# Adding the experts' results for every other sequence on GpSimd in place of TensorE and VectorE, in the last stage of a Mamba and mixture-of-experts block

## The chip, the cores and the metric

The kernel runs on one core of one Trainium2 chip. The metric is the device time of one execution in microseconds (us), as the median over several runs. A profile is one further execution, recorded by the hardware profiler; its span runs from the first to the last instruction of the program, and its times are counted from the span's start. The core has five engines with a queue of instructions each: TensorE (PE; the loads of its weights appear as PEld), VectorE (DVE), ScalarE (ACT), GpSimd (POOL) and SyncE (SP). SP, ACT and POOL also issue DMAs.

## The reference

The input x has 8 sequences of 512 tokens with 128 channels. The block has two halves: an attention-like part of four Mamba-2 layers, and a feed-forward part with a shared expert and eight routed experts of which each token takes two. Each half is modulated by vectors made from a condition c.

```python
h = _layernorm(x, axis=-1) * (1 + ca) + sa
x = x + ga * _L0_attn_ref(h, ...)              # four Mamba-2 layers
h = _layernorm(x, axis=-1) * (1 + cb) + sb
x = x + gb * _L0_ffn_ref(h, ...)               # experts

# in _L0_ffn_ref
shared = jnp.maximum(normed @ sw1 + sb1, 0.0) @ sw2 + sb2
scores, idx = jax.lax.top_k(probs, TOPK)       # two experts of eight for each token
w = scores / (jnp.sum(scores, axis=-1, keepdims=True) + 1e-06)
...
routed = jnp.einsum('teo,te->to', eo, comb)    # the two experts' results, weighted and added
return shared + routed.reshape(b, s, -1)
```

All values are float32.

## The kernel before, in words

All sequences stay in SBUF as tiles xs[b] of 128 partitions by 4 x 128 values. The Mamba layers come first and take most of the time, with the routing of the first sequences beside the last layer. Each routed token is written as a row to a list of its expert in DRAM (`xg`), once for each of its two experts. Then come 39 tiles of 256 rows each: `fetch` loads the expert's weights and the rows, `turn` transposes them, `hidden` makes the hidden layer, and `combine` makes the expert's result, adds its bias (L1218), multiplies each row by its weight (L1220) and scatters it to a DRAM table `yg` with indirect DMAs of GpSimd (L487). In `yg` the first result of token t stands in row t, its second in row T + t, where T is the number of all tokens. Beside these tiles, `fold` adds the shared expert's part to xs[b] and loads the gate gb of sequence b to `gbs[b]`, 128 values that are the same on every partition.

The last stage begins when the last scatter has landed. For each of the 8 sequences b it loads y1[b] (the first results) by a DMA of SP and y2[b] (the second results) by a DMA of ACT, both 128 x 512 values, 256 KB (L1269). The loads of all sequences are issued ahead of the additions. Two sequences share one tile of the pool `xbp`. After that a second loop goes over the sequences:

- TensorE adds: a matmul of the identity matrix with y1[b], and one with y2[b] on top of it, in one bank of PSUM, `sum2` (L1275, L1276). The pool of banks has three.
- VectorE multiplies the sum in PSUM by gb, broadcast over the four tokens of a partition, and writes the product over y1[b] (L1278).
- VectorE adds the product to xs[b] (L1281).
- SP stores xs[b] to the output (L1282), 256 KB.

The order of instructions on PE, DVE, ACT and SP is the order of the program text, as it stands in this part of the kernel (`tc.manual_schedule` names all engines but Pool). On GpSimd the order is set by the scheduler of the tile framework. Waits between engines come from the framework: an instruction waits for the semaphores of what made its inputs, and each engine runs its own instructions in order. SP therefore issues the stores in the order of the sequences, and a store that waits holds the later ones.

Of the kernel before, what the change touches and what calls it, by code (L numbers as in the profile page):

```python
# [15 lines left out]
P = 128  # L16
# [8 lines left out]
def adaln_mamba_moe(  # L25
# [27 lines left out]
    nc = tc.nc  # L53
    B, L, DM = x.shape
# [4 lines left out]
    NC = L // Q  # L59
# [39 lines left out]
    ident = const.tile([P, P], F32, name="ident")  # L99
# [39 lines left out]
    def step(gen):  # L139

        return gen is not None and next(gen, gen) is not gen
# [71 lines left out]
    hTs, hp, xp, xs = {}, {}, {}, {}  # L213
# [271 lines left out]
    def scatter(to, of, ix, group):  # L485

        i = nc.gpsimd.indirect_dma_start(  # L487
            out=to, out_offset=bass.IndirectOffsetOnAxis(ap=ix, axis=0), in_=of, in_offset=None
        )
        tc.declare_no_dep(i.ins, group=group, reason="the rows that they write are distinct")  # L490
        tc.add_to_no_dep_group(group, i.ins)
# [12 lines left out]
    def pbank(name):  # L504
        return psP.tile([P, 512], F32, tag="p", name=name)
# [61 lines left out]
    def serve():  # L567
        nonlocal serving
        if not step(serving):
            serving = None  # L570

    with ExitStack() as actx:
# [422 lines left out]
        for t in range(-NC * LEAD - EARLY, NI + 4):  # L995
            p = t + NC * LEAD
# [101 lines left out]
    gbs = {}  # L1098
    fgb = ctx.enter_context(tc.tile_pool(name="fgb", bufs=B))

    def fold(b):

        gbs[b] = fgb.tile([P, DM], F32, tag="gb", name=f"gb{b}")
        nc.sync.dma_start(gbs[b], mods[b, 3].partition_broadcast(P))
        yield
        nc.vector.tensor_add(accs[b], accs[b], b2.unsqueeze(1).to_broadcast([P, NC, DM]))
        yield
        nc.vector.tensor_mul(accs[b], accs[b], gbs[b].unsqueeze(1).to_broadcast([P, NC, DM]))
        yield
        nc.vector.tensor_add(xs[b], xs[b], accs[b])  # L1110
# [53 lines left out]
    def fetch(j):  # L1164
        to = tab["to"]
        e = nc.sync.value_load(to[:1, 0, j : j + 1], min_val=0, max_val=E - 1)
        r = nc.sync.value_load(to[:1, 1, j : j + 1], min_val=0, max_val=E * ER)
        w1x[j] = fw3.tile([P, FH], F32, tag="w1", name=f"w1_{j}")
        nc.sync.dma_start(w1x[j], ew1[bass.ds(e, 1)].rearrange("o d h -> d (o h)"))
        w2x[j] = fw3.tile([P, FK, DM], F32, tag="w2", name=f"w2_{j}")  # L1170
        nc.sync.dma_start(w2x[j], ew2[bass.ds(e, 1)].rearrange("o (k p) d -> p (o k) d", p=P))

        b2x[j] = fw3.tile([P, DM], F32, tag="b2", name=f"b2_{j}")
        nc.sync.dma_start(b2x[j], eb2[bass.ds(e, 1)].rearrange("o d -> (o d)").partition_broadcast(P))

        def rest():
            rows_in[j] = fw3.tile([P, 2, RW], F32, tag="rows", name=f"rows{j}")
            nc.sync.dma_start(rows_in[j], xg[bass.ds(r, TT), :].rearrange("(p s) w -> p s w", s=2))

        return rest  # L1180

    def turn(j):
        pt = psT.tile([P, 2, P], F32, tag="t", name=f"pt{j}")
        for s in range(2):
            nc.tensor.transpose(pt[:, s, :], rows_in[j][:, s, :DM], ident)  # L1185
        xts[j] = fh.tile([P, TT], F32, tag="xt", name=f"xt{j}")
        nc.scalar.activation(xts[j], pt.rearrange("p s t -> p (s t)"), AF.Copy, scale=nw)

    def hidden(j):
        hds[j] = hd = fh.tile([P, FK, TT], F32, tag="hd", name=f"hd{j}")  # L1190
        xt, w1 = xts.pop(j), w1x.pop(j)
        for half in range(2):
            ph = pbank(f"ph{j}_{half}").rearrange("p (k t) -> p k t", t=TT)
            ks = range(half * FK // 2, (half + 1) * FK // 2)
            for i, k in enumerate(ks):
                nc.tensor.matmul(ph[:, i, :], w1[:, k * P : (k + 1) * P], xt, start=True, stop=True)  # L1196
            for i, k in enumerate(ks):
                bias = tab["b1"][:, j, k : k + 1]
                if half:
                    nc.vector.tensor_scalar(hd[:, k, :], ph[:, i, :], bias, 0.0, ALU.add, ALU.max)  # L1200
                else:
                    nc.scalar.activation(hd[:, k, :], ph[:, i, :], AF.Relu, bias=bias)  # L1202

    def combine(j):
        hd, w2, rows = hds.pop(j), w2x.pop(j), rows_in.pop(j)
        pe = banks[-1](f"pe{j}")[:, : 2 * DM].rearrange("p (s d) -> p s d", s=2)
        for s in range(2):
            for k in range(FK):
                nc.tensor.matmul(  # L1209
                    pe[:, s, :], hd[:, k, s * P : (s + 1) * P], w2[:, k, :], start=(k == 0), stop=(k == FK - 1)  # L1210
                )
        ix = fh.tile([P, 2], mybir.dt.uint32, tag="ix", name=f"ix_{j}")

        own = fh.tile([P, 2], F32, tag="own", name=f"own{j}")
        nc.vector.tensor_scalar(own, rows[:, :, DM + 1], float(2 * T), float(j * TT), ALU.is_ge, ALU.mult)
        nc.vector.tensor_add(ix, own, rows[:, :, DM + 1])
        y = fh.tile([P, 2, DM], F32, tag="y", name=f"y{j}")
        nc.vector.tensor_add(y, pe, b2x.pop(j).unsqueeze(1).to_broadcast([P, 2, DM]))  # L1218
        for s in range(2):
            nc.vector.tensor_scalar_mul(y[:, s, :], y[:, s, :], rows[:, s, DM : DM + 1])  # L1220
        for s in range(2):
            scatter(yg, y[:, s, :], ix[:, s : s + 1], "results")

    with tc.manual_schedule(engines={*tc.nc.engines} - {mybir.EngineType.Pool}):
        tail = list(gens.values())
        fetched = []
        table = None
        while tail or serving or scatters or table or not tab:
            for g in list(tail):
                if not step(g):  # L1230
                    tail.remove(g)
            while scatters:
                scatter(*scatters.pop(0)[1:])
            serve()
            for g in list(tail):
                if not step(g):
                    tail.remove(g)
            serve()
            if len(taken) == len(sets) + 1 and not tab:
                table = tables()  # L1240
            if not step(table):
                table = None
            if not fetched and "to" in tab:
                fetched = [fetch(j) for j in range(3)]
            serve()
        for rest in fetched:
            rest()
        turn(0)
        turn(1)
        hidden(0)  # L1250
        folding = [fold(b) for b in range(B)]
        for j in range(NT):
            if j + 3 < NT:
                fetch(j + 3)()
            if j + 1 < NT:
                hidden(j + 1)
            if j + 2 < NT:
                turn(j + 2)
            combine(j)
            if folding and not step(folding[0]):  # L1260
                del folding[0]

        y1, y2 = {}, {}
        for b in range(B):
            both = xbp.tile([P, NX, L], F32, tag="xbc", name=f"y{b}") if b % 2 == 0 else both
            for c, (eng, y) in enumerate(((nc.sync, y1), (nc.scalar, y2))):
                y[b] = both[:, 2 * (b % 2) + c, :]
                r = c * T + b * L
                eng.dma_start(  # L1269
                    y[b].rearrange("p (s d) -> p s d", d=DM),  # L1270
                    yg[r : r + L, :].rearrange("(p s) d -> p s d", s=NC),
                )
        for b in range(B):
            sum2 = pbank(f"sum{b}")
            nc.tensor.matmul(sum2, ident, y1[b], start=True, stop=False)  # L1275
            nc.tensor.matmul(sum2, ident, y2[b], start=False, stop=True)  # L1276
            y = y1[b].rearrange("p (s d) -> p s d", d=DM)
            nc.vector.tensor_mul(  # L1278
                y, sum2.rearrange("p (s d) -> p s d", d=DM), gbs[b].unsqueeze(1).to_broadcast([P, NC, DM])
            )  # L1280
            nc.vector.tensor_add(xs[b], xs[b], y)  # L1281
            nc.sync.dma_start(out[b].rearrange("(s p) d -> p s d", p=P), xs[b])  # L1282


# [49 lines left out]
```

## Time and profile before

| | |
|---|---|
| median of 3 runs | 1150.44 us (1149.92 to 1153.31) |
| the profiled execution | 1151.86 us |
| its span | 1150.2 us (1150.15 unrounded) |
| granted TensorE clock, mean | 0.93 |
| busy: PE, DVE, ACT, POOL | 967.3, 859.0, 761.5, 856.3 us |
| last scatter issued / first y load issued | 1122.60 / 1124.85 |
| first sum begins / last x ready | 1129.57 / 1146.76 |
| loads of y, stores of x in the last stage | 16 and 8, of 256 KB each |

A profile's busy time is that of the whole span; what the change touches is the last 25 us, so it is read in windows, in the chain of waits (which is followed backwards from the last instruction to whatever released each one) and in the timeline of single instructions. The groups of instructions give counts and mean durations, and a group's line names the engine, the operation, output<-inputs and their shapes.

### The profile page before, as it was taken

The page shows a single profiled execution, that of the slowest core. Times are in us where ns is not written, and L with a number is a line of the kernel's source. Part 1 is how long each engine was busy: PE and PEld are TensorE (multiplying, and loading weights), DVE is VectorE, ACT ScalarE, POOL GpSimd, SP SyncE. Part 2 cuts the span into 40 slices and gives each one's busy share as a digit, 9 for nine tenths or more (in the row PEclk, how much of TensorE's full clock was granted, in tenths as well). Part 3 has the DMA queues.
Part 4 walks back from the last instruction along what each step waited for, and adds up shares of the span by engine and source line. Part 5 has one row for each costly group of instructions (what it writes and reads, how often), then busy time and mean ns, then how long its engine had stood idle before and what let it go on. Part 6 is the DMA issues. An engine that isn't in the chain of part 4 may idle for free. (4 is left out here: it accounts for less than half of the span.)

```text
span 1150.2 us, 21566 instructions
## 1 busy us (share of the span) xinstructions
PE 967.3 (84%) x7130; PEld 732.4 (64%) x7130; DVE 859.0 (75%) x2084; ACT 761.5 (66%) x1641; POOL 856.3 (74%) x937
## 2 busy tenths in 40 slices
PE   3666899989999989999998999879664994999995
PEld 1234666767677667676676676657453674888882
DVE  2858888888988888888889888887764652666653
ACT  3766888878898788888978887876534741333320
POOL 6858879888898798988988988989666163555550
PEclk9777989999999999999999999986886896999998
DMA  5131436455475454653432433423201015788856
GB/s 110 4 128 49 136 98 195 130 157 176 112 227 153 127 183 135 184 170 100 128 109 88 140 109 125 134 91 129 85 27 37 9 45 160 222 231 224 220 145 226
DMA packets 134302, 151.19 MB, mean 131 GB/s; under 512 B 22568, under 2 KB 106696, under 8 KB 134192
## 3 DMA queue, kind: packets, MB, share of 16 engines
q1 hardware_dynamic: 127184, 137.91, 40.6%
q0 software_dynamic: 4672, 9.42, 2.4%
q10 hardware_dynamic: 2336, 2.50, 0.7%
q8 instruction: 56, 0.92, 0.3%
q14 instruction: 54, 0.44, 0.1%
HBM read 120.07 MB, written 29.71 MB: 130 GB/s over the span
## 5 line engine op out<-in xcount | busy, mean ns | idle before, releaser
L662 DVE SCALAR_TENSOR_TENSOR xbc<-px,cw,xbc 128x511 f32<-128x511 f32 (+2 forms) x384 | 286.2, 745 | 36.4 <-ACT xbc L652 29.3
L795 POOL TENSOR_TENSOR dV<-dV,cum 128x1024 f32<-128x1024 f32 x128 | 243.8, 1905 | 5.5 <-DMA dV<-crow 5.5
L854 DVE TENSOR_TENSOR dV<-dV,ptx 128x1024 f32<-128x1024 f32 x128 | 155.1, 1211 | 18.7 <-ACT xT L832 18.7
L800 POOL TENSOR_SCALAR_AFFINE_SELECT dV<-dV 128x1024 f32<-128x1024 f32 x128 | 142.6, 1114 | 9.3
L811 ACT ACTIVATE dV<-dV 128x1024 f32<-128x1024 f32 x128 | 134.5, 1051 | 15.6 <-POOL dV L800 15.3
L487 POOL DMA_INDIRECT yg<-y,ix x78 | 84.1, 1079 | 79.3 <-DVE y L1220 64.7
L938 ACT ACTIVATE sq<-g 128x256 f32<-128x256 f32 x128 | 53.0, 414 | 119.5 <-DVE g L934 105.6
L640 PE MATMUL px<-hT,Wi 128*128 128x512 f32 x192 | 104.9, 629 | 15.8 <-DVE xbc L662 14.5
L652 ACT ACTIVATE xbc<-px,cbias,cw 128x512 f32<-128x512 f32 x128 | 98.4, 769 | 23.3 <-PE px L640 21.9
L838 POOL TENSOR_TENSOR xd<-xT,dt 128x256 f32<-128x256 f32 x128 | 79.5, 621 | 29.4 <-ACT xT L832 28.8
L487 POOL DMA_INDIRECT xg<-row,ix x64 | 63.3, 990 | 50.4 <-ACT hds L523 29.7
L863 PEld LDWEIGHTS py<-xbc,st 128*128 128x128 f32 x384 | 60.3, 204 | 60.6 <-issue 47.4
L953 PE MATMUL po<-Wo,g 128*128 128x128 f32 x512 | 88.9, 297 | 0.0
L1202 ACT ACTIVATE hd<-ph,bs 128x256 f32<-128x256 f32 x78 | 32.7, 470 | 84.1 <-PE ph L1196 81.7
L922 PE MATMUL py<-dV,xd 128*32 128x128 f32 x2048 | 84.5, 284 | 0.0
L949 PEld LDWEIGHTS po<-ones,sq 128*128 128x128 f32 x512 | 67.7, 192 | 26.1 <-issue 23.2
L912 PEld LDWEIGHTS py<-xbc,dg 128*128 128x128 f32 x512 | 79.3, 201 | 7.0 <-issue 1.0
L850 PE MATMUL ptx<-xbc 128*128 128x128 f32 x256 | 56.0, 301 | 32.6 <-DVE dV L854 32.0
L912 PE MATMUL py<-xbc,dg 128*128 128x128 f32 x512 | 81.4, 284 | 0.0
L949 PE MATMUL po<-ones,sq 128*128 128x1 f32 x512 | 78.2, 257 | 0.5 <-ACT sq L938 0.5
L1209 PE MATMUL pe<-w,hd 128*128 128x128 f32 x624 | 75.9, 275 | 0.0
L1196 PE MATMUL ph<-xt,w 128*128 128x256 f32 x312 | 75.8, 388 | 0.0
(252 smaller groups left out, 2348.8 us busy)
## 6 DMA issues: line engine op xcount, KB each, us to landing
dV<-crow SPq DMA_DIRECT2D x128, 512.0 KB, 4.0
w<-in_L_ffn_ew_dram SPq DMA_DIRECT2D x78, 256.0 KB, 3.5
xg<-blank SPq DMA_DIRECT2D x64, 260.0 KB, 4.7
ecum<-crow SPq DMA_DIRECT2D x256, 48.0 KB, 3.2
rows<-xg SPq DMA_DIRECT2D x39, 130.0 KB, 3.2
b<-in_L_ffn_eb_dram SPq DMA_DIRECT2D x39, 64.0 KB, 4.5
x<-in_L_attn_x_dram SPq DMA_DIRECT2D x8, 256.0 KB, 5.4
md<-mods SPq DMA_DIRECT2D x8, 256.0 KB, 4.9
```

Of the source, the lines that this page charges most:

```text
L487: i = nc.gpsimd.indirect_dma_start(out=to, out_offset=bass.IndirectOffsetOnAxis(ap=ix, axis=0), in_=of, in_offset=None)
L640: nc.tensor.matmul(px[v, k][:, :L], Wi[l][:, c0 : c0 + P], hT[v], start=True, stop=True)
L652: nc.scalar.activation(xbc[v][:, k, :], px[v, k][:, :L], AF.Identity, bias=cbias[:, l, k : k + 1], scale=cw[:, l, k, KT - 1 : KT],)
L662: nc.vector.scalar_tensor_tensor(xbc[v][:, k, d:], px[v, k][:, : L - d], cw[:, l, k, KT - 1 - d : KT - d], xbc[v][:, k, d:], ALU.mult, ALU ...
L795: nc.gpsimd.tensor_tensor(dV[i], dV[i], cums[g][:, h0 : h0 + NH].unsqueeze(2).to_broadcast([P, NH, Q]), ALU.subtract)
L800: nc.gpsimd.affine_select(out=dV[i], in_=dV[i], pattern=[[0, NH], [1, Q]], compare_op=ALU.is_ge, fill=-200.0, base=0, channel_multiplier=-1,)
L811: nc.scalar.activation(dV[i], dV[i], AF.Exp)
L854: nc.vector.tensor_mul(Ms[i], Ms[i], pg.pop(i).unsqueeze(1).to_broadcast([P, NH, Q]))
L912: nc.tensor.matmul(py[i][:, k, :], dg[l][:, k, :], xbc[u][:, k, t], start=False, stop=True, skip_group_check=True,)
L922: nc.tensor.matmul(py[i][j * HD : (j + 1) * HD, k, :], xd[:, h, :], M[:, h, :], start=False, stop=True, skip_group_check=True,)
L949: nc.tensor.matmul(pp[:, 2 * DM + c : 2 * DM + c + 1], sq[:, k, :], ones[:, 0:1], start=(k == 0), stop=(k == NB - 1))
L953: nc.tensor.matmul(pp[:, c * DM : (c + 1) * DM], g[:, k, :], Wo[l][:, k, :], start=(k == 0), stop=(k == NB - 1))
```

## The change

For odd b, TensorE does nothing any more. GpSimd adds y2[b] to y1[b] in SBUF, VectorE multiplies y1[b] in place by gb, and GpSimd adds the product to xs[b]. For even b all stays as it was. The store on SP is the same for both.

```diff
         for b in range(B):
-            sum2 = pbank(f"sum{b}")
-            nc.tensor.matmul(sum2, ident, y1[b], start=True, stop=False)
-            nc.tensor.matmul(sum2, ident, y2[b], start=False, stop=True)
             y = y1[b].rearrange("p (s d) -> p s d", d=DM)
-            nc.vector.tensor_mul(
-                y, sum2.rearrange("p (s d) -> p s d", d=DM), gbs[b].unsqueeze(1).to_broadcast([P, NC, DM])
-            )
-            nc.vector.tensor_add(xs[b], xs[b], y)
+            gb = gbs[b].unsqueeze(1).to_broadcast([P, NC, DM])
+            if b % 2:
+
+                nc.gpsimd.tensor_add(y1[b], y1[b], y2[b])
+                nc.vector.tensor_mul(y, y, gb)
+                nc.gpsimd.tensor_add(xs[b], xs[b], y)
+            else:
+                sum2 = pbank(f"sum{b}")
+                nc.tensor.matmul(sum2, ident, y1[b], start=True, stop=False)
+                nc.tensor.matmul(sum2, ident, y2[b], start=False, stop=True)
+                nc.vector.tensor_mul(y, sum2.rearrange("p (s d) -> p s d", d=DM), gb)
+                nc.vector.tensor_add(xs[b], xs[b], y)
             nc.sync.dma_start(out[b].rearrange("(s p) d -> p s d", p=P), xs[b])
```

In the program that is built from this, GpSimd's eight new instructions stand at the end of its queue: the four additions of y2 to y1 (b = 1, 3, 5, 7) first, then the four additions to xs in the same order. VectorE's are in the order of the sequences: multiplication and addition for an even b, the multiplication alone for an odd one. The rest of the program has the same instructions in the same order on every engine.

## The prediction

> **What bounds the kernel now.** I read the page first, then the chain of waits near the end, then the end in windows and by instruction. Times are us from the span's start, rounded to 0.05 in sums. Here is the end of the chain:
>
> ```profile
> 1129.57 2.08 PE sum L1275 x2
> 1131.64 1.65 PE sum L1276 x2
> ...
> 1143.59 0.86 PE sum L1275 x2
> 1144.45 0.87 PE sum L1276 x2
> 1145.32 0.03 issue
> 1145.35 0.70 DVE y L1278
> 1146.05 0.03 issue
> 1146.07 0.69 DVE x L1281
> ```
>
> From 1129.57, when the first pair y1, y2 is there, the end is TensorE's: 0.86 + 0.86 = 1.72 a sequence (3.73 for the first). VectorE adds 1.44 after the last sum, and the final store with the end of the program 3.4 more (1150.15 less 1146.76).
>
> The windows (us; busy PE, PEld, DVE, ACT, POOL; clock; DMA share; GB/s) show what lies beside this:
>
> ```profile
> 1133.00:1135.00 2.00, 2.00 (x6) 0.92 (x5) 1.38 (x2) 0.00 (x0) 0.00 (x0) 0.97 1.05 392
> 1135.00:1137.00 2.00, 2.00 (x7) 0.80 (x6) 1.62 (x3) 0.00 (x0) 0.00 (x0) 1.00 1.05 395
> 1137.00:1139.00 2.00, 2.00 (x6) 0.94 (x5) 1.67 (x3) 0.00 (x0) 0.00 (x0) 1.00 1.06 345
> 1139.00:1141.00 2.00, 2.00 (x6) 0.91 (x5) 1.63 (x4) 0.00 (x0) 0.00 (x0) 1.00 0.66 201
> ```
>
> PE is full, DVE nearly so, POOL idle, and the loads of y run at about 394 GB/s, 0.524 MB a pair: one pair each 1.33, so pair b lands near 1129.5 + 1.33b. The DMA events agree: pairs 1, 3, 5, 7 at 1130.75, 1133.55, 1136.25, 1138.8. Without TensorE's pace the loads would be the limit, up to 8 earlier than the end at 1146.76.
>
> The prices of the moved work are in the groups, where the end of a line is busy us, mean ns, idle before:
>
> ```profile
> L185 POOL TENSOR_TENSOR h<-h,mdA 128x512 f32<-128x512 f32 x4 | 5.0, 1260 | 0.2
> L1281 DVE TENSOR_TENSOR x<-x,y 128x512 f32<-128x512 f32 x8 | 5.5, 692 | 0.3
> L1278 DVE TENSOR_TENSOR y<-sum,gb 128x512 f32<-128x512 f32 x8 | 5.5, 691 | 14.9 <-PE sum L1276 14.0 <-DMA y<-yg 0.6 <-DMA out_dram<-x 0.3
> ```
>
> How POOL and DVE go together is in the timeline, where both are busy (start, us, engine):
>
> ```profile
> 88.80 1.89 POOL L795 TENSOR_TENSOR dV<-dV,cum 128x1024 f32<-128x1024 f32 x1
> ...
> 89.69 1.54 DVE L185 TENSOR_TENSOR h<-h,mdA 128x512 f32<-128x512 f32 x1
> 90.76 1.42 POOL L800 TENSOR_SCALAR_AFFINE_SELECT dV<-dV 128x1024 f32<-128x1024 f32 x1
> 91.27 1.46 DVE L186 TENSOR_TENSOR h<-h,mdA 128x512 f32<-128x512 f32 x1
> 92.16 1.04 POOL L838 TENSOR_TENSOR xd<-xT,dt 128x256 f32<-128x256 f32 x1
> ```
>
> The DVE operation, 0.69 alone, ends 0.54 after POOL's (90.69 to 91.23); POOL's next, 1.11 on average, ends 0.95 after that; then 0.55 on DVE, then 0.47 on POOL for a 0.62 operation. They take turns, and each holds the other off, less 0.14.
>
> **What the Trainium skill says.** "SBUF — State Buffer", section "Who interferes with whom": a VectorE instruction with two SBUF inputs and a GpSimd one that reads SBUF exclude each other for a whole instruction; with one SBUF input VectorE doesn't contend. The lines above agree: 1.54 in place of 0.69. "GPSIMD Engine Reference", section "3.1 Elementwise — side-by-side cycle accounting", has about 2.6 cycles an element at 1.2 GHz, so an estimate of 1.1 for 512 elements and dispatch beyond; the trace has 1.26, which I use. "TensorE: Matmul & The Clock Gate", section "What's actually happening": full clock after some 3.4 us of work. Here it is 0.50 until 1133 and 1.00 later; the first sum stays cold after the change too, since nothing ahead of it moves.
>
> **The change, part by part.** The instruction order of the changed program is the old one up to the end; the differences are these. PE loses the sums of 1, 3, 5, 7 (4 x 1.72 = 6.9). DVE loses their four adds to x (2.8) and keeps the multiplications, whose inputs are now both in SBUF. POOL gets eight adds, 8 x 1.26 = 10.1, in this order: y of 1, 3, 5, 7, only then x of 1, 3, 5, 7. SP keeps its stores in sequence order, so store 1 now waits for POOL's fifth add, with stores 2 to 7 behind it. Loads are issued as before.
>
> Walked through with m for the multiplication, a for DVE's add, y and x for POOL's adds:
>
> PE: sum 0 at 1133.3 as now, sum 2 at 1135.0, sum 4 at 1136.7, sum 6 at 1137.6 (its pair lands) + 1.72 = 1139.3. None holds anything later than 1139.3, so 6.9 of TensorE goes off the path.
>
> POOL, first four: y1 1130.8 to 1132.05; y3 1133.6 to 1134.85; y5 1136.3 to 1137.55; y7 1138.85 to 1140.15. Each waits for its pair.
>
> DVE: m0 1133.35 to 1134.0; a0 has two SBUF inputs and meets y3: 1134.85 + 0.54 = 1135.4; m1 to 1136.1; m2 to 1136.85; a2 meets y5: 1137.55 + 0.54 = 1138.1; m3 to 1138.85; m4 (PSUM, no exclusion) to 1139.55; a4 meets y7: 1140.15 + 0.54 = 1140.7.
>
> From there the two take turns, POOL at 1.26 - 0.14 = 1.12 behind a DVE operation and DVE at 0.54 behind POOL's: x1 1141.8, m5 1142.35, x3 1143.45 (m6 from PSUM runs beside it), a6 1144.0, x5 1145.1, m7 1145.65. x7 needs m7 and meets nobody: 0.07 + 1.26 = **1147.0**. Now the last x is ready at 1146.76: **+0.25**. In words: TensorE's chain is replaced by one of five POOL adds and four DVE operations that exclude each other, behind a pair that lands at 1138.8.
>
> Store 7 is issued at once and costs the 3.4 that it costs now. The other stores: 1 and 2 go at 1141.85 and 1142.3, 3 and 4 from 1143.5, 5 and 6 from 1145.15. Alone, stores move 311 GB/s (window 1138 to 1140), 0.85 each; store 7 of before ends its packets about 1.9 after its issue, so data begin some 0.95 after issue. Seven in a row from 1142.8 end at 1148.75, and store 7 by itself at 1147.05 + 1.9 = 1148.95: hidden, with 0.2 of room.
>
> So the span goes from 1150.15 to 1150.4. The profiled execution took 1151.86 (1.7 outside the span); the median of the runs is 1150.44, 1.4 lower, and I add the 0.25 to that: **1150.7**.
>
> **Costs that no row shows.** POOL adding two full tensors at the end, with loads beside it, isn't in the trace. Lower bound: no exclusion at all, where POOL alone decides: y7 ends 1140.15, then 4 x 1.33 = 1145.5, **-1.3**. Upper: full durations in the turns, nine operations, 5 x 1.26 + 4 x 0.69 and 8 gaps of 0.06 from 1138.87: 1148.4, **+1.6**. I take the turns as measured. POOL's start after 7 us of rest: under 0.1 in any row; if more, y1 has 3 us to spare.
>
> **The rivals.** *Faster, POOL-adds cheaper:* an add at DVE's 0.69 without exclusion would leave DVE's own order: m6 after sum 6 to 1140.05, a6 1140.75, m7 1141.5, x7 1142.25, 4.5 earlier (1146). Against it, 1260 ns in every 128x512 row of POOL. *No exclusion:* -1.3, 1149.1; the timeline speaks against it. *Slower, the stores:* held behind store 1 until 1141.85, seven stores must go in a row. At s us each their data end at 1142.8 + 7s, before at 1148.7; this decides from 0.9, and costs over 0.3% (3.45) from s = 1.35, that is 194 GB/s. For it, the 173 GB/s of the windows after 1141; against it, those were paced by DVE's 1.72 a store, and 311 was reached when two were queued. At s = 1.4: +3.9, 1154.3. *The change takes work from an engine that did not hold the end:* not so, since PE runs its 16 matmul pairs without a gap and DVE waits for it.
>
> **How the numbers follow.** 0.3% (3.45 us) is about what a measurement of this kernel can tell from no change. The forecast of turns: 0.65. No exclusion: 0.15; both lie within 0.3%. Cheaper adds or a gain I don't see: 0.10. Stores, or exclusion dearer than any row: 0.10. So faster 0.10, same 0.80, slower 0.10. The bounds -1.3 and +1.6, and 0.6 either way since the three runs shown differ by more than the effect, give 1148.8 to 1152.9, taken as 1148.7 to 1152.9.
>
> **What would show it.** DVE adds of about 1.1 to 1.35 where 0.69 stood (a0, a2, a4, a6), POOL x adds of about 1.6; POOL's last add ending near 1147.0; PE idle from 1139.3; SP's store 1 near 1141.85, behind POOL x. Wrong if DVE's adds stay at 0.69 and POOL's x adds at 1.26 (no exclusion), if POOL's last add ends ahead of 1143.5, or if the last store ends over 2.5 after its issue.

## The result, and the profile after

| | before | after |
|---|---|---|
| median of 22 runs each | 1149.72 us (1145.32 to 1153.31) | 1152.64 us (1148.62 to 1158.17) |
| ratio to before | | 1.003, 95% interval 1.0016 to 1.0045 |
| first load of y issued | 1124.85 | 1118.96 |
| last x ready, from that load | 21.91 | 22.11 |
| last x to the end of the span | 3.39 | 6.54 |
| first load of y to the end of the span | 25.30 | 28.64 |

The change made the kernel slower by 0.3 per cent where no change was forecast. The profiled execution of after has the shorter span, 1147.6 us against 1150.2: its last stage began 5.9 us earlier, in a part of the program with the same instructions. Across all profiles shown here that moment lies between 1118.96 and 1126.53, so the spans say little, and from here on a stage is measured **from the issue of its first load of y**. Counted so, the last stage costs 3.34 us more, which is 0.29 per cent of 1149.72 and lies within the interval of the runs (0.16 to 0.45).

The chain of waits of after, its last pieces (start us, us, what):

```profile
1132.91 1.27 POOL y L1278
1134.18 5.00 POOL x L1280 x3
1139.18 0.59 issue
1139.77 1.29 POOLq L1335
```

The last x is now GpSimd's. The last name is POOL's sequencer at L1335, the line where the framework closes the program. The chain of before ended with VectorE's last addition and named no store either, so the chain alone doesn't say what fills the time behind the last x. The groups of instructions in the last stage (busy us, mean ns, idle before):

```profile
L1280 POOL TENSOR_TENSOR x<-x,y 128x512 f32<-128x512 f32 x4 | 6.3, 1596 | 0.6 <-DVE y L1279 0.6
...
L1286 DVE TENSOR_TENSOR x<-x,y 128x512 f32<-128x512 f32 x4 | 5.3, 1337 | 0.1
L1278 POOL TENSOR_TENSOR y<-y 128x512 f32<-128x512 f32 x4 | 5.1, 1263 | 11.5 <-DMA y<-yg 11.5
...
L1279 DVE TENSOR_TENSOR y<-y,gb 128x512 f32<-128x512 f32 x4 | 4.8, 1212 | 0.0
L1285 DVE TENSOR_TENSOR y<-sum,gb 128x512 f32<-128x512 f32 x4 | 2.7, 681 | 12.6 <-PE sum L1284 12.6
```

VectorE's additions, with two SBUF inputs, went from 692 ns to 1337 on average. Its multiplications took 691 when one input was in PSUM; those that now have both in SBUF take 1212, and those that still read PSUM take 681. The timeline shows the turns one by one:

```profile
1132.91 1.27 POOL L1278 TENSOR_TENSOR y<-y 128x512 f32<-128x512 f32 x1 [1.45 <-DMA y<-yg]
...
1133.25 1.48 DVE L1286 TENSOR_TENSOR x<-x,y 128x512 f32<-128x512 f32 x1
1134.13 5.05 POOL L1280 TENSOR_TENSOR x<-x,y 128x512 f32<-128x512 f32 x3
1134.65 1.75 DVE L1279 TENSOR_TENSOR y<-y,gb 128x512 f32<-128x512 f32 x1
1136.31 0.68 DVE L1285 TENSOR_TENSOR y<-sum,gb 128x512 f32<-128x512 f32 x1
1137.03 1.04 DVE L1286 TENSOR_TENSOR x<-x,y 128x512 f32<-128x512 f32 x1
1137.98 1.74 DVE L1279 TENSOR_TENSOR y<-y,gb 128x512 f32<-128x512 f32 x1
1139.81 1.26 POOL L1280 TENSOR_TENSOR x<-x,y 128x512 f32<-128x512 f32 x1 [0.63 <-DVE y L1279]
```

POOL's y7 (the addition of y2 to y1 for sequence 7) ends at 1134.18, VectorE's addition 0.55 later, POOL's x1 1.1 after that, and so on; the last addition ends at 1141.07, which is 22.11 after the first load. Up to here the walk through the prediction holds: counted from the first load, the turns from y7 on end within 0.1 us of it, and the last x within 0.05. What comes after it does not. Windows of after (us; busy PE, PEld, DVE, ACT, POOL; clock; DMA share; GB/s):

```profile
1139.00:1141.07 2.07, 0.00 (x0) 0.00 (x0) 0.73 (x1) 0.00 (x0) 1.44 (x2) 0.50 0.99 290
1141.07:1143.90 2.83, 0.00 (x0) 0.00 (x0) 0.00 (x0) 0.00 (x0) 0.00 (x0) 0.50 0.72 219
1143.90:1147.60 3.70, 0.00 (x0) 0.00 (x0) 0.00 (x0) 0.00 (x0) 0.00 (x0) 0.50 0.00 0
```

The stores are done at 1143.9. For 3.7 us more nothing is computed and nothing is moved. Each engine closes the program with DRAIN instructions, and the engines then signal each other by semaphores. The instructions of the closing line tell what is waited for. This is the view of that line in before, then in after (count, then ns min/median/max, then the first and the last start in us):

```profile
L1330 POOLq EVENT_SEMAPHORE  x4: 17/17/17, 1149.3 to 1150.0; - x4
L1330 POOLq DRAIN  x3: 51/103/8313, 1120.9 to 1149.8; - x3
L1330 SPq DRAIN  x3: 7/7/7, 1149.2 to 1149.5; - x3
```

```profile
L1335 POOLq EVENT_SEMAPHORE  x4: 17/17/17, 1146.8 to 1147.5; - x4
L1335 POOLq DRAIN  x3: 51/103/6943, 1139.8 to 1147.3; - x3
L1335 SPq DRAIN  x3: 7/7/7, 1143.9 to 1147.0; - x3
```

POOL's first drain, the longest of its three, ends at 1120.9 + 8.3 = 1129.2 in before and at 1139.8 + 6.9 = 1146.7 in after. POOL's last operation ended at 1123.56 and at 1141.07: **the drain ends 5.63 and 5.65 us after GpSimd's last operation.** In before that was long over when the last store landed; in after SP is through with its stores at 1143.9 and has to wait for POOL until 1146.7. POOL's first closing semaphore instruction shows the same turn: in before it comes at 1149.3, right behind SP's drain at 1149.2, in after at 1146.8, right behind POOL's own. Some 0.9 us of common closing follow in both.

### The profile page after: what moved, and what is told of

It is laid out like the page before. It is cut to its first block, busy times and chain, and to the rows that moved or that the text cites. A ratio compares the mean times of both kernels' runs of the same rounds, so it can differ in the third digit from the quotient of the medians.

```text
span 1147.6 us, 21540 instructions
## 1 busy us (share of the span) xinstructions
PE 958.5 (84%) x7114; PEld 728.3 (63%) x7114; DVE 858.6 (75%) x2080; ACT 762.0 (66%) x1641; POOL 868.0 (76%) x945
```

## The experiments

The theory is that of the **drain**: the program ends 0.9 after the later of two, SP's last landed store and POOL's drain, and the drain ends 5.65 after whatever GpSimd did last. The rivals: the **stores**, which in after stand behind store 1 and go in a bunch; **exclusion**, GpSimd and VectorE holding each other off, as the thing that costs; and **any GpSimd work** in the last stage, wherever it stands. All numbers below but the ratio are us from the issue of the first load of y, in the profiled execution. "Drain" is when POOL's drain ends, "SP" when SP has seen the last store land.

| | last x | last POOL operation | drain | SP | end of span | ratio to before, 95% interval |
|---|---|---|---|---|---|---|
| before | 21.91 | -1.29 | 4.34 | 24.37 | 25.30 | |
| the change | 22.11 | 22.11 | 27.75 | 24.90 | 28.64 | 1.003 (1.0016 to 1.0045) |
| POOL adds y alone | 21.03 | 15.17 | 20.82 | 23.48 | 24.42 | 0.9985 (0.9966 to 1.0003) |
| before + touch of the last x | 21.63 | 22.00 | 27.64 | 24.09 | 28.54 | 1.0012 (0.9994 to 1.003) |
| before + touch of the sixth x | 22.21 | 19.14 | 24.79 | 24.66 | 25.68 | 1.0004 (0.9987 to 1.002) |
| the change, even products in PSUM | 21.16 | 21.16 | 26.80 | 25.06 | 27.69 | 1.0009 (0.9993 to 1.0025) |
| sequences 1 and 3 on POOL | 19.16 | 14.63 | 20.28 | 21.62 | 22.55 | 0.9959 (0.9941 to 0.9976) |
| the same, other products in PSUM | 18.65 | 13.80 | 19.45 | 21.11 | 22.04 | 0.9975 (0.9956 to 0.9993) |

In every row with POOL work the drain ends 5.65 after the last POOL operation, and in every row of the table the span ends about 0.9 (0.88 to 0.94) after the later of drain and SP. The last column has the whole time, whose earlier part varies by several us. The difference of the stage, as a share of the whole, lies in the interval of each row (for sequences 1 and 3 on its edge), but only the rows of the change and of the last two have an interval without 1.

**The additions to x back on VectorE.**

```diff
-                nc.gpsimd.tensor_add(xs[b], xs[b], y)
+                nc.vector.tensor_add(xs[b], xs[b], y)
```

> GpSimd keeps the four additions of y2 to y1; the four additions to x go back to VectorE. Measured from the issue of the first load of y to the end of the span: 25.3 us before, 28.6 with the whole change. The drain theory (the program ends no earlier than 6.5 after GpSimd's last instruction, 5.65 of it GpSimd's own drain) expects GpSimd's last addition some 8 us ahead of the end, the drain hidden, the last x about 0.2 earlier than before and 25.1 in all: time as before, or up to 0.3 less. The theory that the bunched stores cost it expects 25 to 25.5 too, since stores are even again. The theory that GpSimd and VectorE holding each other off cost it expects about 27, as three of the four exclusions stay.

The end came at 24.42, with the drain over 2.7 before SP: the tail is 3.39 again. That takes away 4.2 of the change's 28.64, though POOL still does half of its work, so GpSimd's presence in the stage is not what costs, and neither is exclusion, which expected about 27. It doesn't tell the drain from the stores, as both are undone. The last x, at 21.03, came 0.7 ahead of what was expected: three of VectorE's operations waited for POOL, as expected, but from 15.65 on its four pairs of multiplication and addition ran at 1.33 each where I had taken 1.44. That is 0.4 of it; the rest isn't traced.

**A touch behind the last x, in the kernel of before.** Nothing else is changed; y1 is no longer needed there, and no one waits for this addition.

```diff
             nc.sync.dma_start(out[b].rearrange("(s p) d -> p s d", p=P), xs[b])
+            if b == B - 1:
+                nc.gpsimd.tensor_add(y1[b][:, 0:1], xs[b][:, 0, 0:1], xs[b][:, 0, 1:2])
```

> The kernel before, and one GpSimd addition of 128x1 that reads the last x when VectorE has made it; nothing waits for it. The drain theory expects GpSimd's last instruction to end 0.2 after the last x and the span 6.5 after that: 28.6 from the first load of y in place of 25.3, some 3.2 us more in the time, with stores, TensorE and VectorE as before. The stores theory and the exclusion theory expect no change (under 0.2).

This is the run that decides between the drain and its rivals. From its timeline, its windows and its closing line:

```profile
1148.34 0.19 POOL L1284 TENSOR_TENSOR y<-x 128x1 f32<-128x1 f32 x1 [23.10 <-DVE x L1281]
```

```profile
1148.53:1150.70 2.17, 0.00 (x0) 0.00 (x0) 0.00 (x0) 0.00 (x0) 0.00 (x0) 1.00 0.39 121
1150.70:1155.07 4.37, 0.00 (x0) 0.00 (x0) 0.00 (x0) 0.00 (x0) 0.00 (x0) 0.64 0.00 0
```

```profile
L1332 POOLq DRAIN  x3: 51/103/5868, 1148.3 to 1154.7; - x3
```

An addition of 0.19 us on 128x1 values makes the end of the span 28.54 from the first load in place of 25.30, with stores as evenly spaced as in before and no 128x512 operation on POOL. Its drain begins at 1148.3, takes 5.87 and ends 5.65 after the touch. For the last 4.4 us no engine computes and the DMA stands still. The stores and exclusion theories expected nothing here. The whole time rose by 0.12 per cent with an interval that holds both 0 and the 0.28 expected: where the earlier part of the program varies by several us, the medians of this run don't settle 3 us. What settles it is the stage in the one profiled execution.

**The same touch behind the sixth x.**

```diff
+            if b == 5:
+                nc.gpsimd.tensor_add(y1[b][:, 0:1], xs[b][:, 0, 0:1], xs[b][:, 0, 1:2])
```

> The same small GpSimd addition, but behind x of the sixth sequence (b = 5), which is ready 3.4 us earlier. The drain theory expects the drain to end just as the last store has landed: 0 to 0.2 us more than before. A theory that any GpSimd work in the last stage costs some 3 us, wherever it stands, expects 3 us more.

The drain ended at 24.79, SP at 24.66: a draw, with the drain later by 0.13. The tail from the last x was 3.47 in place of 3.39. GpSimd work that ends 3.1 us ahead of the last x costs under 0.1, so it isn't GpSimd work as such that costs, but its place.

**The even products left in PSUM.** VectorE writes its product over the sum and adds it to x from there.

```diff
-                nc.vector.tensor_mul(y, sum2.rearrange("p (s d) -> p s d", d=DM), gb)
-                nc.vector.tensor_add(xs[b], xs[b], y)
+                s3 = sum2.rearrange("p (s d) -> p s d", d=DM)
+                nc.vector.tensor_mul(s3, s3, gb)
+                nc.vector.tensor_add(xs[b], xs[b], s3)
```

> The whole change, but for even sequences VectorE leaves its product in the PSUM bank and adds it to x from there, so that its addition has one SBUF input and doesn't meet GpSimd. Exclusion as read from the trace of before expects VectorE's even additions at 0.69 in place of 1.04 to 1.53, while the odd multiplications still wait; GpSimd's last addition about 0.85 earlier than with the whole change. The drain theory expects all of this to be paid back at the end: 27.8 from the first load of y, 2.5 more than before. The stores theory expects little change from the whole change (28.3 to 28.6), as the second store still waits for GpSimd's fifth addition.

Its timeline, where VectorE's addition runs beside POOL's:

```profile
1130.43 1.27 POOL L1278 TENSOR_TENSOR y<-y 128x512 f32<-128x512 f32 x1 [1.32 <-DMA y<-yg]
1130.93 0.69 DVE L1287 TENSOR_TENSOR x<-x,sum 128x512 f32<-128x512 f32 x1
...
1135.90 1.27 POOL L1278 TENSOR_TENSOR y<-y 128x512 f32<-128x512 f32 x1 [1.40 <-DMA y<-yg]
1136.30 1.42 DVE L1279 TENSOR_TENSOR y<-y,gb 128x512 f32<-128x512 f32 x1
```

With one input in PSUM the addition takes 0.69 though POOL works under it; the multiplication with two SBUF inputs still takes 1.42. POOL's last addition came at 21.16, 0.95 earlier than with the whole change (0.85 expected), and the end at 27.69 (27.8 expected): the last x earlier than before, the stage 2.4 longer. So the exclusion of VectorE's even additions is real and worth about 1 us here, and the odd multiplications still wait; with a last x that is earlier than before, what makes the stage longer is the drain. The stores theory expected 28.3 to 28.6.

**GpSimd for sequences 1 and 3 alone.**

```diff
-            if b % 2:
+            if b in (1, 3):
```

> GpSimd takes sequences 1 and 3 alone (both additions), TensorE and VectorE the other six. The drain theory expects GpSimd's last addition some 15 us after the first load of y, its drain over at 21 and hidden; the end is then VectorE's, with 14 operations and up to three that wait for GpSimd: last x at 20.0 in place of 21.9, and 3.4 more to the end of the span, so 23.4 in place of 25.3 before and 28.6 with the whole change, about 0.15 per cent less than before. The theory that any GpSimd addition in the last stage costs 3 us at the end expects 26.5.

The drain ended at 20.28 and was hidden; the last x came at 19.16 and the end at 22.55, 2.75 earlier than before. That is 0.85 ahead of the 23.4 expected; three of VectorE's operations waited, as expected, and its last pairs again ran at 1.33. The time fell to 0.9959 of before. This beats both kernels. The stage explains 0.24 per cent, the lower edge of the interval (0.24 to 0.59); the rest isn't explained by anything in the profile, and I take it for scatter.

**The same, and the other six products in PSUM** (the edit is that of the even products, above).

> As with sequences 1 and 3 on GpSimd, and the even and the other odd products stay in the PSUM bank, so that only the two multiplications of sequences 1 and 3 on VectorE have two SBUF inputs. Exclusion expects nearly every VectorE operation at 0.69, last x 18.5 us after the first load of y, where TensorE's six sums (3.7 + 5 x 1.72) and 1.44 of VectorE also end; drain hidden; end of the span at 21.9, 3.4 us (0.3 per cent) less than before and 6.7 less than the whole change. If VectorE's operations on PSUM are dearer or the stores can't follow, 22.5 to 23.4.

The last x came at 18.65 and the end at 22.04, the shortest stage of all, 3.26 less than before; TensorE's sums and two VectorE operations set it, as expected. The time was 0.9975 of before, with an interval of 0.9956 to 0.9993. Against the version without PSUM the stage is 0.51 shorter; the times of the two have overlapping intervals and don't rank them.

## Why the prediction was wrong, point by point

- **TensorE's 6.9 us off the path: right.** PE's last sum ended ahead of 1134.1 in after, 7 us before the last x.
- **The turns of POOL and VectorE: right.** The last x was 0.20 later than before, counted from the first load, where 0.25 was forecast. The three of POOL's x additions that met VectorE took 1.71 where about 1.6 was forecast, VectorE's additions 1.04 to 1.53 where 1.1 to 1.35 was. What the Trainium skill states in "SBUF — State Buffer", section "Who interferes with whom", agrees with these traces: beside GpSimd, VectorE took longer with two SBUF inputs, and with one it stayed at 0.68 to 0.70. The rival without exclusion fell.
- **"Store 7 is issued at once and costs the 3.4 that it costs now": this step failed.** The 3.4 was taken for the price of the last x, whoever makes it. It is the price of a store at whose end GpSimd has long drained. With GpSimd as the last engine, the tail is its drain and the common closing: 5.65 + 0.89 = 6.54 where the sum had 3.39, that is 3.15 more. With the 0.20 of the later x this is the 3.34 measured, to 0.01. The trace of before showed it, in a line of 8313 ns whose end lies 5.63 after the last scatter; I didn't price the closing of the program for an engine that hadn't been late there.
- **The stores hidden with 0.2 of room: off by a little, without effect.** They went in a bunch at 281 to 290 GB/s, not 311, so 0.90 to 0.93 a store in place of 0.85, and SP was through at 24.90, 0.53 later than before, 0.33 of it beyond the later x. The drain hides that, as it ends at 27.75. The slower rival named the right side for a wrong reason.
- **The chance of 0.10 for slower** covered stores and dearer exclusion, with no place for a cost behind the last store. The median, 1152.64, lies inside the stated range; the forecast of no change did not hold.

## What to carry to other kernels

Ask of each engine not only when its work is needed but when its last work ends. In this kernel, work on GpSimd was free at the end as long as its drain was over before SP had seen the last store land; what the drain lacked beyond that was added to the stage. As an estimate from the runs, SP sees the last store 2.46 us after the last x (24.37 less 21.91) and the drain takes 5.65, so GpSimd had to be done some 3.2 us ahead of the last x. Sharing the stage made it shorter where GpSimd's last addition came early (14 to 15 us after the first load), and longer where it made the last x. And a value that VectorE read back from PSUM instead of SBUF kept it clear of GpSimd.

## What the runs showed of the hardware

- GpSimd's drain at the close of the program ended 5.63 to 5.65 us after its last operation in all eight profiles, be it a scatter (before), an addition of 128x512 (1.26 us) or one of 128x1 (0.19 us). VectorE's ended 0.05 after its last operation in before. What GpSimd does in that time, and whether it has to do with the scatters that this kernel issues from it, was not tried.
- In the view of waits of after, the idle time of SP at the end is put down to PE's sequencer (3.0 us), which had drained at 1134.1; it is GpSimd's. The ends of the drains tell it, the named engine doesn't.
- VectorE's pairs of multiplication and addition, with inputs ready, ran at 1.33 a pair, less than twice 0.69.
